# A statically ordered 32-unit graph kernel: due dates for every engine, first rows on TensorE, idle products before and between the first ones

**Chip, cores, metric.** One core of one Trainium2 chip.

## The reference

```python
# x (64, 256, 128) f32, adj (256, 256) of 0 and 1; four layers, each: x = layernorm(x + layer(x))
# layer 0, 1: attention over the graph
h = x @ W;  e = leaky(u1[i] + u2[j]);  att = softmax(masked e);  out = att @ h   # (+ x @ self_weight, or elu)
# layer 2: five gated steps
m = adj @ h
z = sigmoid(av @ w3.T + h @ u3.T + b);  r = sigmoid(av @ w4.T + h @ u3.T + b)    # av = [m, m]
h = (1 - z) * h + z * tanh(av @ w5.T + (r * h) @ u5.T + b)
# layer 3: x, adj x, adj^2 x, adj^3 x (twice), each times its own weight, summed
```

All products are in f32. A step of layer 2 needs the step before it, so one unit alone leaves TensorE waiting for ScalarE (ACT) and VectorE (DVE); many units at once fill it.

## The kernel before

Two of the 64 graphs make a unit, so there are 32; seven are in work at a time, each in a "lane" of buffers. The kernel doesn't emit instructions in program order. It notes every operation as a task with an engine, a guessed duration and its dependences, plays them through a small list scheduler, and emits each engine's instructions in the order that comes out. On the chip each engine then follows its order, whatever really happens.

```python
LATENCY = {"pe": 500, "dve": 400, "act": 400, "pool": 500, "sp": 4000}       # the planner's guesses, ns
# Plan.run, at each moment of planned time
            for e, tasks in ready.items():
                if free[e] > now:
                    continue
                fit = [t for t in tasks if t.at <= now and len(t.takes) <= len(self.free_banks)]
                if not fit:
                    continue
                t = min(fit, key=key)
# ... cut ...
    def first(t):                                  # the key: the oldest unit first
        if t.rank is not None:
            return (0, t.rank)
        late = t.unit - (NU - LANES)
        if late >= 0 and t.layer > 1:
            return (1, t.step + late * LEAD)
        return (0, t.unit - (LANES if t.layer < 2 and t.unit >= LANES else 0))
```

Layers 0 and 1 need a row of 512 numbers on all partitions. Units 0 and 1 make it with TensorE; later ones send it to DRAM and read it back. Likewise a "far" unit turns its state between steps by DVE in 32x32 blocks and by DRAM; a near one (0, 1 and the last) by TensorE.

```python
    def far(u):
        return DIRECT <= u < NU - NEAR             # DIRECT = 2, NEAR = 1
    def on_all(u, t, row, src, view):
        if u >= DIRECT:
            to_row(row, src, view, G)              # SBUF to DRAM
            from_row(t, row)                       # DRAM to all partitions
            return t, ...
        ps = bank()
        for g in range(G):
            add(PE, 110, lambda g=g: nc.tensor.transpose(...))
        return ps, ...
```

The softmax here doesn't subtract the row's maximum and nothing guards it: scores larger than these inputs give would overflow.

## Time and profile before

| | kernel before |
|---|---|
| median of 3 runs | 1450.38 us (1449.82 to 1453.53) |
| PE records, share of the span busy | 5617, 98% |
| streaming work of these records | 1399.3 us |
| lost in the first 60 us | 23.8 us |
| lost from 60 us to the last matmul | 18.5 us |
| from the last matmul to the end | 6.6 us |

How to read it: an f32 product stands in the trace as two records (a transpose as one). In a full stream a record of N columns takes N/1.2 + 2.1 ns (512: 429 ns, 256: 215 ns), read off from start to start; a one-column record 0.10 us. The streaming work is all records by this price, and "lost" is a stretch of the span less the work in it. Cutting a stretch at an edge makes an error of up to half a us. I call this the stage account; idle products are not counted as work. In the lines, PEld is TensorE's weight load, POOL is GpSimd, SP the engine that issues most DMAs, L-numbers are lines of that run's kernel.py; ps is a PSUM bank, in which TensorE puts its results, and esd a small tile of layer 0 from which layer 1 makes its row. (The prediction's 24.5 and 49 were an earlier, coarser count of the 23.8 and 48.9.) The lines of the profile are in the prediction. This one is the first product of a layer 2 on PE's timeline (start, duration, group):

```profile
59.00 1.12 PE L695 MATMUL ps<-xT,gT 128*128 128x512 f32 x2
```

### The profile page before, as it was taken

Reading aid. Unit: us, or ns where it says so; the run is one execution under the profiler, and the core shown is the slowest. Engines: PE = TensorE matmul, PEld = TensorE weight load, DVE = VectorE, ACT = ScalarE, POOL = GpSimd, SP = SyncE. Lnnn points to the kernel's source line nnn. Section 1 sums busy time; section 2 is a strip of 40 time slices with the busy share of each in tenths; the row PEclk is TensorE's granted clock in tenths of the full one; section 3 lists DMA queues with packets and bytes.
Section 4 is the critical chain, followed back from the end, with each engine's and each line's share of the span. In section 5 each row is a group of like instructions: output and inputs, shape, how many; then the busy total and the mean of one; then the engine's idle time right before and its main releaser. Section 6 shows DMA issues by size and latency. Waiting matters only on the chain.

```text
span 1448.2 us, 18393 instructions
## 1 busy us (share of the span) xinstructions
PE 1416.8 (98%) x5617; PEld 952.5 (66%) x5617; DVE 1116.6 (77%) x2598; ACT 724.5 (50%) x1372; POOL 144.8 (10%) x134
## 2 busy tenths in 40 slices
PE   7899999999999999999999999999999999999998
PEld 6565766566667666666666666666666666665666
DVE  6965788678886887878897887888778888767665
ACT  5664375445553645545544545455455445554431
POOL 0100101001011010010111000111000101000011
PEclk9999999999999999999999999999999999999999
DMA  6201334545455435554544545453554454443232
GB/s 149 47 22 30 73 81 102 119 100 115 98 118 127 96 89 114 118 122 98 110 106 110 112 92 126 105 111 86 122 116 90 106 107 99 96 106 80 66 95 66
DMA packets 516162, 142.12 MB, mean 98 GB/s; under 512 B 446176, under 2 KB 482272, under 8 KB 516064
## 3 DMA queue, kind: packets, MB, share of 16 engines
q1 hardware_dynamic: 515264, 140.42, 43.4%
q8 instruction: 45, 0.74, 0.2%
q10 hardware_dynamic: 800, 0.52, 0.1%
q14 instruction: 53, 0.43, 0.1%
HBM read 79.01 MB, written 61.85 MB: 97 GB/s over the span
## 4 chain that ended last, share of the span: by engine, by line
PE 92%; DVE 4%; ACT 2%; DMA 1%; issue 1%; SPq 1%; POOLq 0%; POOL 0%; DVEq 0%; ACTq 0%
PE ps L695 45%; PE ps L675 22%; PE ps L781 8%; PE ps L637 4%; PE ps L788 4%; PE ps L607 3%; PE ps L540 2%; PE ps L651 2%; PE ps L602 2%; DMA u<-rowu 0%; PE ps L750 0%; ACT p L585 0%; DVE st L500 0%; PE ps L447 0%; ACT e L626 0%
## 5 line engine op out<-in xcount | busy, mean ns | idle before, releaser
L695 PE MATMUL ps<-m,gT 128*128 128x512 f32 x960 | 462.0, 594 | 3.6 <-ACT m L691 2.9
L695 PEld LDWEIGHTS ps<-m,gT 128*128 128x128 f32 x960 | 177.5, 190 | 163.8 <-issue 136.6
L505 POOL TENSOR_TENSOR rstd<-ve,nhalf 128x4 f32<-128x4 f32 x128 | 144.1, 1128 | 1298.2 <-DVE ve L502 1152.6
L675 PE MATMUL ps<-adjTp,ht 128*128 128x256 f32 x928 | 230.6, 379 | 0.6 <-DVE x L510 0.6
L675 PEld LDWEIGHTS ps<-adjTp,ht 128*128 128x128 f32 x928 | 175.0, 190 | 79.5 <-issue 58.4
L714 DVE TENSOR_TENSOR p<-p,xT 128x512 f32<-128x512 f32 x160 | 109.6, 685 | 110.5 <-ACT p L708 110.2
L710 ACT ACTIVATE e<-ps,bias 128x512 f32<-128x512 f32 x160 | 109.8, 687 | 147.9 <-PE ps L695 147.9
L701 ACT ACTIVATE e<-ps,bias 128x512 f32<-128x512 f32 x160 | 109.8, 687 | 115.2 <-PE ps L695 114.8
L691 ACT COPY m<-ps 128x512 f32<-128x512 f32 x160 | 93.3, 584 | 145.5 <-PE ps L675 142.8
L695 PE MATMUL ps<-e,u5T 128*128 128x512 f32 x320 | 162.5, 593 | 0.2
L695 PE MATMUL ps<-xT,gT 128*128 128x512 f32 x320 | 162.0, 593 | 0.6 <-DVE xT L717 0.5
L703 DVE SCALAR_TENSOR_TENSOR e<-e,xT 128x512 f32<-128x512 f32 x160 | 109.4, 685 | 53.9 <-ACT e L701 53.1
L708 ACT ACTIVATE p<-ps,bias 128x512 f32<-128x512 f32 x160 | 109.9, 687 | 64.5 <-PE ps L695 63.4
L675 PE MATMUL ps<-adjT,x 128*128 128x256 f32 x512 | 127.7, 379 | 0.0
L715 DVE SCALAR_TENSOR_TENSOR p<-e,p 128x512 f32<-128x512 f32 x160 | 109.4, 685 | 7.9 <-ACT e L710 5.5
L675 PEld LDWEIGHTS ps<-adjT,x 128*128 128x128 f32 x512 | 95.4, 191 | 30.3 <-issue 19.2
L717 DVE SCALAR_TENSOR_TENSOR xT<-p,xT 128x512 f32<-128x512 f32 x160 | 109.3, 685 | 2.5
L695 PEld LDWEIGHTS ps<-e,u5T 128*128 128x128 f32 x320 | 60.0, 190 | 54.7 <-issue 44.4
L500 DVE BATCH_NORM_STATS2 st<-ps 128x6 f32<-128x256 f32 x128 | 53.7, 426 | 54.8 <-PE ps L788 44.3
L695 PEld LDWEIGHTS ps<-xT,gT 128*128 128x128 f32 x320 | 59.1, 190 | 43.1 <-issue 30.2
L626 ACT ACTIVATE e<-m,esd 128x256 f32<-128x256 f32 x120 | 86.8, 761 | 0.0
L725 DVE STREAM_TRANSPOSE p<-xT 128x512 f32<-128x512 f32 x116 | 81.6, 705 | 1.4
(137 smaller groups left out, 1841.4 us busy)
## 6 DMA issues: line engine op xcount, KB each, us to landing
hb<-p SPq DMA_DIRECT2D x174, 256.0 KB, 2.1
ht<-hb SPq DMA_DIRECT2D x464, 64.0 KB, 2.5
m<-row SPq DMA_DIRECT2D x60, 256.0 KB, 3.7
xT<-hb SPq DMA_DIRECT2D x232, 64.0 KB, 2.5
out_dram<-x SPq DMA_DIRECT2D x32, 256.0 KB, 2.3
hb<-p SPq DMA_DIRECT2D x116, 64.0 KB, 1.8
ht<-hb SPq DMA_DIRECT2D x29, 256.0 KB, 2.9
z<-in_x_dram SPq DMA_DIRECT2D x100, 64.0 KB, 2.4
```

The costliest lines, as they stand in the source:

```text
L505: add(POOL, 1050, lambda: nc.gpsimd.tensor_tensor(rstd.ap, ve.ap, nhalf.ap, op=ALU.pow), (ve, nhalf), (rstd,))
L675: add(PE, mm_ns(N), lambda b=b, mc=mc: nc.tensor.matmul(ps.ap[:, b * N : (b + 1) * N], lhs(b, mc), mat.ap[:, mc, :], start=(mc == 0), stop ...
L691: add(ACT, 500, lambda ps_m=ps_m: nc.scalar.copy(m.ap, ps_m.ap), (ps_m,), (m,))
L695: add(PE, mm_ns(T), lambda: nc.tensor.matmul(ps.ap, w(), rhs.ap, start=start, stop=stop, skip_group_check=True), (c, rhs), (ps,))
L701: add(ACT, 600, lambda ps_g=ps_g: nc.scalar.activation(r.ap, ps_g.ap, AF.Tanh, bias=bias2.ap[:, 1:2], scale=0.5), (ps_g, bias2), (r,))
L703: add(DVE, 600, lambda h=h: nc.vector.scalar_tensor_tensor(r.ap, r.ap, 1.0, h.ap, op0=ALU.add, op1=ALU.mult), (r, h), (r,))
L708: add(ACT, 600, lambda ps_v=ps_v: nc.scalar.activation(v.ap, ps_v.ap, AF.Tanh, bias=bias2.ap[:, 2:3]), (ps_v, bias2), (v,))
L710: add(ACT, 600, lambda ps_g=ps_g: nc.scalar.activation(z.ap, ps_g.ap, AF.Tanh, bias=bias2.ap[:, 0:1], scale=0.5), (ps_g, bias2), (z,))
L714: add(DVE, 600, lambda h=h: nc.vector.tensor_sub(v.ap, v.ap, h.ap), (v, h), (v,))
L715: add(DVE, 600, lambda: nc.vector.scalar_tensor_tensor(v.ap, z.ap, 1.0, v.ap, op0=ALU.add, op1=ALU.mult), (v, z), (v,))
L717: add(DVE, 600, lambda h=h, new=new: nc.vector.scalar_tensor_tensor(new.ap, v.ap, 0.5, h.ap, op0=ALU.mult, op1=ALU.add), (v, h), (new,))
L781: add(PE, mm_ns(N), lambda k=k, src=src, c=c, b=b: nc.tensor.matmul(view(c)[:, :, b, :], bn(src.ap)[:, b, c * P : (c + 1) * P], w3.ap[:, k ...
```

## The change

The intent: order all engines by due dates, so that units keep an even distance and none starves, and close ranks at the end; give the first units a straighter way (rows, loads, constants); keep TensorE's clock up with idle products; tell the planner which writes to one tile don't wait for each other.

```diff
-NEAR = 1
+NEAR = 2
+PERIOD = 43e3
+TAIL = 0.1
+PACE = 1.9
+PACE_GATED = 1.56
+HOLD = 80
+DIRECT_ROWS = 4
@@ Plan.run: a due date for each task of a new unit
+                for t in self.tasks[seen:]:
+                    t.due = max([d.due + (PACE_GATED if t.layer == 2 else PACE) * (d.ns + (
+                        d.wait + self.LATENCY["sp" if d.dma else d.eng] if d.dma or d.eng != t.eng else self.OWN[t.eng]))
+                        for d in t.deps if d.unit == t.unit], default=0.0)
@@ first(t): the key
-        late = t.unit - (NU - LANES)
-        if late >= 0 and t.layer > 1:
-            return (1, t.step + late * LEAD)
-        return (0, t.unit - (LANES if t.layer < 2 and t.unit >= LANES else 0))
+        if t.unit < 0:
+            return t.due - 1e6
+        return (t.unit - (1 - TAIL) * max(t.unit - (NU - LANES), 0)) * PERIOD + t.due
@@ loads: x of unit 0 first on ACT's queue, ahead of adj; x of units 7 to 13 later
-            if not k and u + LANES < NU:
-                load_x(u + LANES)
+            if k == (1 if u < LANES else 0) and u + LANES < NU:
+                load_x(u + LANES, after=[plan.tasks[-1]] if k else ())
@@ rows of units 2 and 3 by TensorE
-        if u >= DIRECT:
+        if u >= DIRECT_ROWS:
@@ idle products, ident by ident, 256 columns: four at the start, six in layer 1 of unit 0 at the lowest priority
+    warm(4)
+            warm(6, [plan.tasks[-1]])
@@ in thirteen places: writes of pieces of one tile are one group
-                (e, nm), (p, s))
+                (e, nm), (p, s), group=ps_)
... HOLD, waits of loads and the order of constants cut ...
```

## The prediction

> **What bounds the kernel now.** I read the page's busy table first, then the stages, then PE's waits, then the engines that PE waits for.
>
> ```profile
> PE 1416.8 (98%) x5617; PEld 952.5 (66%) x5617; DVE 1116.6 (77%) x2598; ACT 724.5 (50%) x1372; POOL 144.8 (10%) x134
> PE 92%; DVE 4%; ACT 2%; DMA 1%; issue 1%; SPq 1%; POOLq 0%; POOL 0%; DVEq 0%; ACTq 0%
> ```
>
> TensorE is the bound: 98% busy, and 92% of the chain that ended last. But busy spans of matmuls overlap, so I price the stream by its cadence. The timeline of PE in mid-kernel gives it (start, duration, group, count):
>
> ```profile
> 601.40 3.62 PE L675 MATMUL ps<-adjTp,ht 128*128 128x256 f32 x16
> 604.86 3.60 PE L695 MATMUL ps<-m,gT 128*128 128x512 f32 x8
> 608.29 1.07 PE L540 MATMUL ps<-wx,xT 128*128 128x133 f32 x8
> ```
>
> From start to start, a record of 512 columns takes (608.29-604.86)/8 = 0.429 us, one of 256 takes 3.46/16 = 0.216, one of about 130 takes 0.112. Transposes in a run of 13 near 17 us are 0.109 apart. The groups by form count 1600 records of 512, 2568 of 256, 1280 of 129 to 133, some 150 transposes and small ones, 16 of one column (0.10 each): 686 + 553 + 142 + 16 + 2 = 1399 us of pure streaming. The span is 1448.2, so **49 us are lost**, and only those can be won. Where, the stages say (columns: window, length, then busy us and counts of PE, PEld, DVE, ACT, POOL, then clock, DMA share, GB/s):
>
> ```profile
> 0.00:10.00 10.00, 5.75 (x30) 5.63 (x31) 4.00 (x18) 3.53 (x5) 0.70 (x6) 1.00 0.72 197
> 10.00:30.00 20.00, 19.10 (x165) 18.22 (x163) 15.61 (x67) 11.56 (x39) 1.02 (x1) 1.00 0.62 130
> 30.00:60.00 30.00, 17.76 (x97) 14.31 (x98) 25.97 (x85) 15.17 (x44) 4.40 (x4) 0.83 0.42 75
> 60.00:100.00 40.00, 40.00 (x171) 26.68 (x170) 29.00 (x71) 28.09 (x57) 3.19 (x3) 1.00 0.06 21
> 100.00:1200.00 1100.00, 1092.65 (x4269) 727.77 (x4268) 873.85 (x1999) 557.25 (x1040) 111.21 (x99) 1.00 0.46 103
> 1200.00:1440.00 240.00, 239.97 (x887) 158.79 (x887) 164.06 (x351) 108.92 (x190) 22.24 (x19) 1.00 0.38 88
> 1440.00:1448.20 8.20, 1.59 (x8) 1.06 (x6) 4.14 (x13) 0.00 (x0) 2.02 (x2) 0.80 0.21 65
> ```
>
> Pricing each stage's records with the cadences, I get 35.5 us of work in the first 60 (24.5 lost), about 18.5 lost from 60 to 1440 (nearly all of it between 140 and 1200, in gaps under 1 us), and 6.6 from the last matmul to the end. From 1200 to 1440 nothing is lost, so the old order already ends full. The start is the largest piece, and its waits have names:
>
> ```profile
> PE ps L490 <- DVE esd L612: 5.4, 2, 5.1
> PE ps L303 <- DMA adj_t<-in_adj_dram: 4.2, 1, 4.2
> PE ps L447 <- DVE x L514: 3.9, 2, 3.4
> PE ps L637 <- DVE p L630: 2.4, 2, 1.9
> ```
>
> Behind the 5.1 us wait at 30 us stands a DMA. The waits of DVE and of ACT up to 60 us, and the chain there:
>
> ```profile
> DVE d L559 <- DMA u<-rowu: 3.0, 2, 2.5
> ...
> ACT p L585 <- DVE nm L583: 6.4, 2, 3.3
> ...
> 29.87 4.36 DMA u<-rowu
> ```
>
> The rows of units 2 and 3 go out to DRAM and come back. The SP queue puts them among the loads of later units, they land late, DVE stands before unit 3's small sum with the last step of unit 2's maximum behind it, ACT stands before unit 2's softmax, which needs that maximum, and unit 0's ready exponential waits behind that on ACT (it starts at 35.10, its inputs were there at 31.46). So the first unit reaches layer 2, where TensorE's work is, only at 54 us.
>
> **What the Trainium skill says.** (1) "TensorE: Matmul & The Clock Gate", Part 1: the array runs at 1.2 GHz by default and at 2.4 after about 3.4 us of sustained work, and one idle window sends it back. The trace agrees: the first transposes are 0.21 us apart until 7.9 us and 0.11 later, and the granted clock is 0.69 from 30 to 35 and 0.50 from 35 to 40, after the gap of 5.1. (2) The same page, Part 2, "Back-to-back issue gap": N/2.4 + 2.5 ns. A record here is two such passes: 512/1.2 + 2.5 = 429 ns, as measured, so steady matmuls have no slack to give. [...]Here a 2 KB row takes 2.4 and the 3.8 KB gather 3.2, so a round trip of two is near 6 us, plus the queue. (4) "Advanced Engine Details and Errata", "Sequencer Loop": queued instructions wait for their semaphores. The trace shows what that costs when the order is wrong: the exponential above.
>
> **The change part by part.** The arithmetic of 29 units is untouched; only order moves.
>
> *Added PE work.* NEAR 2 lets unit 30 turn by PE instead of by DVE and DRAM: two turns of 4 transposes and five steps of 4, 28 x 0.109 = 3.1 us. DIRECT_ROWS 4 makes the rows of units 2 and 3 by PE: 2 units x 2 rows x 4 = 16 transposes, 1.7 us, and 16 one-column records, 1.6 us. Sum **+6.4 us**, all on the bound engine. The ten idle products are 20 records x 0.216 = 4.3 us at full clock; four come before any data has landed, and six have the lowest rank in the order, so I count them as lying in idle time, +0. PE should count 5617+28+32+20 = 5697 records.
>
> *Taken off the start.* The rows of units 2 and 3 lose 14 SP issues (about 6 us of queue) and both round trips. The loads for units 7 to 13 wait until layer 1 of the lane's unit instead of layer 0. That takes away the 5.1 us wait and the throttle it brings (about 10 us at a half or less, of which the records ran 4 to 5: some 2.5 us). The x load of unit 0 goes ahead of the adjacency on ACT's queue; the first matmul may come no earlier than 4 us, since adjacency still needs 3.4 from issue, so perhaps 0.5 later. Four warm products from about 1.4 us on put the full clock at about 5 to 6 us instead of 7.9: about 1 us. The write groups only let the planner know that pieces of a tile don't wait for each other, so its order fits the chip better; 1 to 2 us on the first unit's chain. A limit stays: layers 0 and 1 cost DVE about 14 us per unit and PE about 6.6, so until the first unit is in layer 2, PE can't be full. If that comes at about 44 instead of 54, PE's loss falls by about the same. I take **24.5 to 14, -10.5 us**.
>
> *Middle.* Due dates with 43 us between units spread seven units over their phases, where the old key let the oldest unit take everything and then starve. The real PE period is 1399/32 = 43.7, so the pace fits. But only 18.5 us are there, in small waits. I take a third to a half: **18.5 to 10.5, -8 us**.
>
> *End.* It was full until the last matmul, and the last statistics, POOL power, four scalings and a store (2.3 us to land) still follow. Unit 30 near gives shorter steps, which the new tail, with units 4.3 us apart, needs; it buys no more than is lost now: **0**.
>
> Sum: 6.4 - 10.5 - 8 + 0 = -12.1 us, so 1450.4 goes to **1438**; I round it down by one for the reach of the clock, **1437 us** (0.9% faster).
>
> **Rivals.** (a) *The added transposes and products eat the gain.* For it: PE is the bound for 1200 us, and every added record there is paid in full. Against: they sum to 6.4, the lost start to 24.5. If the start wins only 5 and the middle nothing: about 1451. (b) *Due dates starve the middle.* For it: durations and latencies are the planner's guesses (a DMA is taken as 4 us), engines run in the order given, and DVE at 79% from 100 to 1200 has little slack; a tail of seven units at once makes DVE wait. Against: the old order used the same guesses and lost 1.7% there. If loss there doubles: 1455 to 1465. (c) *DVE sets the start.* It is 87% busy from 30 to 60 and 100% from 50 to 60, which speaks for it: then removing the DMA wait saves only some 5 us and PE goes on waiting for DVE: 1443. (d) *Everything fits:* start loss 10, middle 4, end 6: 1405 + 20 + 2 of launch = 1427. Even this is not 2%, which would be 1421.4, or all but some 14 us of the lost time gone.
>
> **Range and chances.** The lower end is (d) less a little, the upper end (a): 1426 to 1450. Faster by over 2% needs more than the profile has to give once the added work is paid: 0.05. Slower by over 2% (1479) would need 29 us of new waits in an order that was surely tried: 0.03. Within 2%: 0.92.
>
> **What would show it right or wrong.** Right: PE at about 5697 records; no clock below 0.9 after 10 us; no wait of PE for the esd row over 2 us; the first layer-2 matmul with the 512-column gate weights near 48 instead of 59 us; work in the first 60 us at 44 to 48 us instead of 35.5; PE busy 100 to 1200 at over 1095 of 1100. Wrong: DVE at 100% through 20 to 60 with PE waiting for it (c); new waits of PE for ACT's copies or DVE's new state in the middle (b); PE gaps after 1350, where there were none; idle products standing between real ones (a). A store or a DVE queue at the end longer than 7 us would void the zero there.

## More of the kernel before

Times are device microseconds (us) of one execution, medians of the runs. Runs of one call share a chip and the runs of the kernel before on it.

## The result

1439.39 us median of 4 runs (1438.70 to 1440.57) against 1450.27 of the kernel before: ratio 0.9921, 95% interval 0.9904 to 0.9938. So 0.8% faster, within 2%. (A ratio is the mean time of one kernel's runs over that of the other's of the same rounds, so not quite the ratio of the medians.) The profiled run is the slowest of the four, 1440.57.

Busy time of PE, and the chain that ended last, of the changed kernel:

```profile
PE 1423.5 (99%) x5697; PEld 962.9 (67%) x5697; DVE 1113.1 (77%) x2589; ACT 722.6 (50%) x1378; POOL 143.5 (10%) x134
PE 97%; DVE 1%; ACT 1%; issue 0%; POOL 0%; POOLq 0%; DVEq 0%
```

PE is busy for longer in a shorter span (4.3 us of it are the ten idle products, priced by cadence), and the chain is now 97% PE: DMA has gone from it, and DVE fell from 4% to 1%. The stages (window, length, then busy us and counts of PE, PEld, DVE, ACT, POOL, then clock, DMA share, GB/s):

```profile
0.00:10.00 10.00, 8.64 (x38) 7.72 (x39) 3.85 (x17) 2.94 (x4) 0.70 (x6) 1.00 0.68 193
10.00:30.00 20.00, 19.70 (x173) 19.25 (x172) 17.39 (x69) 12.57 (x39) 1.73 (x2) 1.00 0.24 69
30.00:60.00 30.00, 29.07 (x165) 22.80 (x164) 27.99 (x84) 20.69 (x54) 5.49 (x5) 1.00 0.31 55
...
100.00:1200.00 1100.00, 1094.36 (x4283) 731.45 (x4282) 878.84 (x2012) 554.96 (x1041) 110.86 (x100) 1.00 0.48 105
```

The third line is where the change shows: from 30 to 60 us PE goes from 17.76 busy to 29.07 of 30 (some 2.6 of them the six idle products), and the clock from 0.83 to 1.00. The last has hardly moved (1092.65 before). PE's longest waits over the whole span:

```profile
PE ps L725 <- DVE esd L638: 2.7, 1, 2.7
PE ps L725 <- ACT m L721: 2.0, 3, 0.8
PE ps L663 <- DVE p L656: 1.7, 2, 1.0
PE ps L299 <- POOL ident masks.py:199: 1.4, 1, 1.4
```

The waits for the esd row at 30 us and for the state at 54 are gone, and the one for the adjacency at the start is filled by idle products. From PE's timeline, the idle products (the groups with ident alone as operand) and the first product of a layer 2:

```profile
1.36 3.78 PE L299 MATMUL ps<-ident 128*128 128x256 f32 x8 [1.36 <-POOL ident masks.py:199]
...
35.06 2.75 PE L299 MATMUL ps<-ident 128*128 128x256 f32 x12
38.60 1.99 PE L663 MATMUL ps<-p,x 128*128 128x256 f32 x8 [0.79 <-DVE p L656]
...
47.02 1.02 PE L725 MATMUL ps<-xT,gT 128*128 128x512 f32 x2
```

Layer 2 starts at 47.0 us instead of 59.0. One new thing stands in the middle, the 2.7 us wait of the list above. Timeline and windows of PE there:

```profile
1192.25 1.02 PE L818 MATMUL ps<-e,a2T 128*128 128x256 f32 x4
1195.99 2.08 PE L725 MATMUL ps<-xT,gT 128*128 128x512 f32 x2 [2.72 <-DVE esd L638]
1197.86 1.51 PE L725 MATMUL ps<-m,gT 128*128 128x512 f32 x2
1199.20 1.89 PE L705 MATMUL ps<-adjTp,ht 128*128 128x256 f32 x8
```

```profile
1194.00:1196.00 2.00, 0.01 (x1) 0.01 (x1) 1.35 (x8) 0.00 (x0) 1.68 (x2) 0.85 0.35 88
1196.00:1198.00 2.00, 2.00 (x3) 0.97 (x4) 1.28 (x5) 0.00 (x0) 0.00 (x0) 0.50 0.04 1
```

PE stands 2.7 us until DVE has finished a layer 0 of another unit (its esd is the last reader of that unit's PSUM tile; a replay of the planner, whose order matches PE's records in the trace one by one, gives the waiting product, of unit 28, the very bank that unit 29's layer 0 held before). GpSimd's two powers in a row (1.68 us in the first window) are on the way to it. Then the granted clock is 0.50 and the next four records of 512 columns take 3.21 us instead of 1.72: some 4.2 us for one bad moment of the order. It is no accident of this run: a wait of 2.2 to 2.7 us for esd stands between 1191 and 1199 us in the profiles of experiments 4, 5, 6 and 10 too.

### The profile page after: what moved, and what is told of

It reads as the page before. It is cut to its first block, busy times and chain, and to the rows that moved or that the text cites. A ratio compares the mean times of both kernels' runs of the same rounds, so it can differ in the third digit from the quotient of the medians.

```text
span 1438.8 us, 18453 instructions
## 1 busy us (share of the span) xinstructions
PE 1423.5 (99%) x5697; PEld 962.9 (67%) x5697; DVE 1113.1 (77%) x2589; ACT 722.6 (50%) x1378; POOL 143.5 (10%) x134
## 4 chain that ended last, share of the span: by engine, by line
PE 97%; DVE 1%; ACT 1%; issue 0%; POOL 0%; POOLq 0%; DVEq 0%
PE ps L725 48%; PE ps L705 23%; PE ps L811 8%; PE ps L633 4%; PE ps L663 4%; PE ps L818 4%; PE ps L677 2%; PE ps L628 2%; PE ps L566 2%; PE ps L780 1%; PE ps L471 0%; ACT e L652 0%; DVE st L525 0%; PE ps L299 0%; PE ps L514 0%
## 5 line engine op out<-in xcount | busy, mean ns | idle before, releaser
L705 PE MATMUL ps<-adjTp,ht 128*128 128x256 f32 x896 | 222.6, 379 | 0.0
L705 PEld LDWEIGHTS ps<-adjTp,ht 128*128 128x128 f32 x896 | 169.6, 190 | 62.2 <-issue 40.9
L725 PEld LDWEIGHTS ps<-e,u5T 128*128 128x128 f32 x320 | 59.9, 190 | 38.1 <-issue 26.3
L525 DVE BATCH_NORM_STATS2 st<-ps 128x6 f32<-128x256 f32 x128 | 51.9, 425 | 40.9 <-PE ps L818 21.2
L652 ACT ACTIVATE e<-m,esd 128x256 f32<-128x256 f32 x112 | 80.4, 761 | 0.7 <-DMA m<-row 0.7
L755 DVE STREAM_TRANSPOSE p<-xT 128x512 f32<-128x512 f32 x112 | 78.3, 700 | 1.2
```

Of the source, the lines that this page charges most:

```text
L705: add(PE, mm_ns(N), lambda b=b, mc=mc: nc.tensor.matmul(ps.ap[:, b * N : (b + 1) * N], lhs(b, mc), mat.ap[:, mc, :], start=(mc == 0), stop ...
L725: add(PE, mm_ns(T), lambda: nc.tensor.matmul(ps.ap, w(), rhs.ap, start=start, stop=stop, skip_group_check=True), (c, rhs), (ps,))
```

## The experiments

The stage account of all kernels. "Planner's idle" is the idle time of TensorE between 60 us and its last matmul in the planner's own account, without a chip: I replayed the planner of each kernel for it.

| kernel | median us | ratio to before | work | lost to 60 us | lost 60 to last matmul | of it to 1200 | after it | planner's idle |
|---|---|---|---|---|---|---|---|---|
| before | 1450.38 | 1 | 1399.3 | 23.8 | 18.5 | 16.7 | 6.6 | 36.5 |
| changed | 1439.39 | 0.9921 | 1405.7 | 11.7 | 14.4 | 13.0 | 7.0 | 26.0 |
| 1 old key in the changed | 1470.85 | 1.0129 | 1405.7 | 16.0 | 42.3 | 40.9 | 6.6 | 57.8 |
| 2 new key alone in the old | 1473.66 | 1.0150 | 1399.3 | 24.9 | 41.2 | 8.6 | 6.5 | 63.5 |
| 3 rows of units 2, 3 back | 1460.65 | 1.0060 | 1402.3 | 16.8 | 31.9 | 9.6 | 6.8 | 63.7 |
| 4 no idle products | 1442.78 | 0.9937 | 1405.7 | 13.7 | 14.7 | 12.1 | 7.0 | 26.0 |
| 5 one near unit | 1443.22 | 0.9940 | 1402.6 | 11.2 | 21.1 | 11.2 | 6.4 | 38.6 |
| 6 loads of units 7 to 13 early | 1439.52 | 0.9915 | 1405.7 | 10.8 | 14.3 | 12.1 | 7.0 | 27.1 |
| 7 no groups | 1446.96 | 0.9965 | 1405.7 | 12.5 | 20.1 | 7.4 | 6.6 | 38.1 |
| 8 other constants | 1432.09 | 0.9865 | 1404.0 | 14.0 | 6.2 | 3.5 | 6.7 | 16.1 |
| 9 rows alone in the old | 1461.12 | 1.0059 | 1402.6 | 16.5 | 34.0 | 32.5 | 6.3 | 50.5 |
| 10 pace 1.85 | 1467.34 | 1.0113 | 1405.7 | 11.7 | 49.7 | 11.2 | 6.7 | 67.7 |
| 11 best constants | 1433.52 | 0.9873 | 1405.7 | 10.6 | 7.6 | 4.8 | 7.0 | 10.9 |

The kernel before took 1451.43 in the call of 1 to 4, 1450.89 in that of 5 to 8 and 1452.90 in that of 9 to 11, so kernels of different calls are compared by ratio.

A caution for the whole table: undoing any part gives the planner another problem, and it draws a whole new order. The time of an ablation is therefore not the price of the part. The stage nearest to the part is.

### 1. The old key

```diff
-        return (t.unit - (1 - TAIL) * max(t.unit - (NU - LANES), 0)) * PERIOD + t.due
+        late = t.unit - (NU - LANES)
+        if late >= 0 and t.layer > 1:
+            return (1, t.step + late * LEAD)
+        return (0, t.unit - (LANES if t.layer < 2 and t.unit >= LANES else 0))
```

> The changed kernel with the old priority key put back (oldest unit first), everything else of the change kept. Theory A, the rows and loads of the first units give the start and the key gives only the middle: loss in the first 60 us stays near 12 us (changed kernel 11.7, kernel before 23.8), loss from 60 us to the last matmul goes back from 14.4 to about 18.5, time about 1443. Rival B, the due dates give most of everything: start loss back above 19, time 1449 or more. Rival C, the key does nothing: 1439 within 2.

Measured 1470.85. None of the three had it: the start lies between A and B (16.0), and the middle is far worse than in the kernel before. One window of it, with PE's busy time first:

```profile
60.00:1200.00 1140.00, 1116.87 (x4336) 740.69 (x4337) 885.70 (x2041) 572.90 (x1087) 118.46 (x99) 1.00 0.45 98
```

With everything else of the change in place, the oldest-first key loses 23 us there by busy time alone. So with these parts and constants the key is needed: without it the rest of the change makes the middle worse.

### 2. The new key alone

```diff
 # kernel before, with t.due, PERIOD, TAIL, PACE, PACE_GATED and
+        return (t.unit - (1 - TAIL) * max(t.unit - (NU - LANES), 0)) * PERIOD + t.due
```

> The kernel before with the due dates as its key and nothing else of the change (rows of units 2 and 3 still through DRAM, old loads, no idle products, one near unit). Theory A: start loss stays above 19 us, middle loss 14 or 15, no added PE work, time about 1446. Rival B: start loss near 13, time about 1435 to 1438, faster than the whole change because the 6.4 us of added work are missing. Rival D: the tail of the new key needs the second near unit, then gaps appear after 1400 us and the time is above 1450.

Measured 1473.66, the slowest median of all. The time refutes A and B; D said where to look. Two stages of it:

```profile
60.00:1200.00 1140.00, 1137.91 (x4450) 759.10 (x4449) 895.94 (x2064) 586.81 (x1106) 108.52 (x99) 1.00 0.45 100
...
1350.00:1471.90 121.90, 96.77 (x338) 61.87 (x337) 58.08 (x125) 35.53 (x60) 10.01 (x9) 0.93 0.20 47
```

Up to 1200 us due dates do what they are for: 8.6 us lost instead of the old key's 16.7. Then the last seven units close up and PE stands 25 us in the last 122 (6.5 of them after its last matmul). Its longest waits from 1300 on are for DVE's normalised state (6.4 us), for a turned unit to land from DRAM (5.3) and for DVE's new state (4.2 in three).

```profile
PE ps L683 <- DVE x L522: 6.4, 1, 6.4
PE ps L789 <- DMA xT<-hb: 5.3, 1, 5.3
```

The start is no better than before (24.9). That the missing second near unit is the cause, as D had it, is not shown: experiment 5 has one near unit too and lost 9.9 us after 1200, against 32.6 here.

### 3. Rows of units 2 and 3 through DRAM again

```diff
-DIRECT_ROWS = 4
+DIRECT_ROWS = 2
```

> The changed kernel with the rows of units 2 and 3 through DRAM again. Theory A: start loss rises from 11.7 to 17 or more, 3.3 us of PE work fall away, time about 1442, and a wait of PE for the esd row or of DVE for the gather of over 2 us is back. Rival B or E, the key orders around the DRAM trips, or the later loads alone freed the queue: start loss about 12, time about 1436, so those two direct units were paid for nothing.

Measured 1460.65. The start rose to 16.8, near A's 17. The time is far above A's 1442 because the new order lost 22 us after 1200, which says nothing on rows. No single wait for a row or the gather over 2 us came back, so the mechanism of A is not shown by this run, only its size.

### 4. No idle products

```diff
-    warm(4)
-            warm(6, [plan.tasks[-1]])
+            pass
```

> The changed kernel without its ten idle products. Theory: they hold the clock; without the four the clock comes up about 2 us later (start loss +1), without the six a gap of over 3 us near 35 to 38 us halves the clock for one window of 3.4 us (+1.7): start loss, idle products not counted as work, 11.7 to about 14, time about 1441.5. Rival: nothing on the path runs in those microseconds, time 1439.4 within 1.

Measured 1442.78 (ratio 0.9937 against 0.9921), with 2.0 us more lost at the start and the rest as it was. The size is as the theory said, but the two intervals (0.9921 to 0.9954, 0.9904 to 0.9938) overlap, so it is the trace that shows the mechanism. PE's timeline, and the clock from 40 to 45:

```profile
39.46 2.54 PE L662 MATMUL ps<-p,x 128*128 128x256 f32 x8 [3.37 <-DVE p L655]
```

```profile
40.00:45.00 5.00, 5.00 (x26) 4.66 (x25) 4.50 (x20) 3.21 (x13) 1.32 (x1) 0.66 0.06 3
```

Without the six, PE stands 3.37 us, and the clock is 0.66 of full afterwards. With them it stands 0.79 and runs at 1.00. How much the four at the start help is left to chance: in the profiled run of the changed kernel records go at the full rate from about 7.4 us, in that of experiment 8 too, in those of experiments 6 and 11, with the same four, already at or just after the first real product (4.6 and about 5.0). Without them it was about 10, in the kernel before 7.9. The first real products of the changed kernel and of experiment 11:

```profile
4.93 0.63 PE L342 MATMUL ps<-centre,w 128*128 128x128 f32 x2
4.93 0.42 PE L342 MATMUL ps<-centre,w 128*128 128x128 f32 x2
```

By the clock records of the traces the rise came at 4.2 to 7.6 us in the nine profiled runs with the four, at 7.7 to 10.1 in the four without. At half rate those 3.4 us are up to 1.7 us of loss, so start losses of single profiles that differ by less than that (the 0.8 of experiment 7, say) prove little.

### 5. One near unit

```diff
-NEAR = 2
+NEAR = 1
```

> The changed kernel with only the last unit near, unit 30 turning through DVE and DRAM again. Theory F, the new tail of seven units needs short steps at the end: PE work falls by 3.1 us, start stays 11.7, but PE gaps of 8 to 15 us appear after 1350 us, time about 1446 to 1452, with a wait of PE for a DMA landing (turned unit or its steps). Rival: one near unit is enough, time 1436, the 3.1 us were paid for nothing.

Measured 1443.22. 3.1 us of work fall away and 6.7 come back as loss (after 1200 it rose from 1.4 to 9.9), so the second near unit paid here, by less than I expected; the intervals overlap (0.9923 to 0.9956, 0.9904 to 0.9938), and the order is another, so that it pays in general is not shown. The mechanism was another: not a DMA (PE waited 0.3 us for one) but one gap, for DVE's normalised state:

```profile
1412.40 0.33 PE L471 MATMUL ps<-ident,x 128*128 128x128 f32 x1 [3.21 <-DVE x L539]
```

After it records again took longer than their price until about 1418: some 1.8 us more.

### 6. Loads of units 7 to 13 early

```diff
-            if k == (1 if u < LANES else 0) and u + LANES < NU:
-                load_x(u + LANES, after=[plan.tasks[-1]] if k else ())
+            if not k and u + LANES < NU:
+                load_x(u + LANES)
```

> The changed kernel with the x loads of units 7 to 13 issued after layer 0 of the lane's first unit again, instead of after layer 1. Theory: with the rows of four units made by PE, the SP queue has little to carry before 40 us, so loads in it no longer hold anything up: start loss 11.7 to 13, time 1439 to 1441. Rival, the queue of SP was the cause: start loss 15 or more and a wait of over 2 us for a row, time 1443 or more.

Measured 1439.52, ratio 0.9915: the same as the changed kernel. With the rows off the queue, this part of the change carries nothing.

### 7. No groups

```diff
-                (e, nm), (p, s), group=ps_)
+                (e, nm), (p, s))          # and so in all places
```

> The changed kernel without the groups that tell the planner that pieces of one tile do not wait for each other. No instruction changes, only the order that comes out. Theory G: an order planned with false waits loses on the chip: start loss 14 to 15, middle loss up by 5 to 10 us, time 1446 to 1452. Rival: the order hardly differs, 1439 to 1441.

Measured 1446.96. Not one instruction differs from the changed kernel's, only their order. The start lost 0.8 more, less than I expected, the rest 5.7 more. G holds in size for time and middle.

### 8. Other constants

```diff
-PERIOD = 43e3
-TAIL = 0.1
-PACE = 1.9
-PACE_GATED = 1.56
-DIRECT_ROWS = 4
+PERIOD = 43.5e3
+TAIL = 0.3
+PACE = 1.7
+PACE_GATED = 1.66
+DIRECT_ROWS = 3
```

> The changed kernel with other constants of the due dates: 43.5 us between units, tail 0.3, pace 1.7, gated pace 1.66, rows of three units direct. Chosen because in the planner's own account TensorE idles less in the middle (16 us against 26) and 2.5 us more at the start; 1.7 us of PE work fall away. Theory H, in 60 us to the last matmul the planner's account ranks orders as the chip does: middle loss 14.4 falls to about 8, start loss 11.7 rises to about 14, time about 1434 to 1436, faster than both kernels. Rival, the planner's account is fitted to the constants it has and the chip's own waits decide: 1440 to 1450.

Measured 1432.09, ratio 0.9865: faster than both kernels, and by more than the theory asked. Middle loss 6.2 instead of 14.4, start 14.0. The same window as in 1 and 2:

```profile
60.00:1200.00 1140.00, 1140.00 (x4467) 762.14 (x4466) 911.74 (x2076) 581.73 (x1099) 110.74 (x102) 1.00 0.47 103
```

PE is never seen idle in 1140 us. The mechanism of the change can do this; the changed kernel's constants didn't.

### 9. Rows alone in the kernel before

```diff
-        if u >= DIRECT:
+        if u >= DIRECT_ROWS:              # 4, in both places
```

> The kernel before with the rows of units 2 and 3 made by TensorE and nothing else of the change. If the rows alone cure the start: start loss 23.8 falls to about 14. If rows and key are both needed (undoing either in the changed kernel gave 16 to 17, the key alone gave nothing): start loss 17 to 21. The wait of PE for the esd row (5.1 us in the kernel before) should be under 2 us in both cases. Middle loss is expected to get worse, since the planner's own account of this order has 50 us of idle TensorE there against 36 for the kernel before: 25 to 35 us, so the time is 1452 to 1462.

Measured 1461.12. Start 16.5, slightly better than "both needed" said: rows alone give 7.3 of the 12.1 us. The longest wait for the esd row fell from 5.1 to 2.2 us, just above the 2 that I had named. The middle got worse as the planner's account said (34.0).

```profile
PE ps L491 <- DVE esd L613: 3.2, 2, 2.2
```

### 10. Pace 1.85

```diff
-PACE = 1.9
+PACE = 1.85
```

> The changed kernel with one constant changed by 3 per cent: pace 1.85 for 1.9. No instruction is added or removed. Theory H: the order is sensitive to its constants and the planner's account shows it (68 us of idle TensorE in the middle against 26): middle loss 35 to 45 us instead of 14.4, start 11.7 as before, time 1460 to 1472, slower than the kernel before. Rival: the due dates as such carry the gain, a small change of pace leaves 1438 to 1444.

Measured 1467.34, from 1463.55 to 1475.47, the profiled run being the slowest. The same start (11.7), the same loss to 1200 (11.2), and some 38 us lost in the last lap. PE's longest wait in total, all of it there, is for DVE's new state:

```profile
PE ps L780 <- DVE xT L747: 11.5, 4, 3.0
```

A constant changed by 3% turns 0.8% faster into 1.1% slower. Middle loss was even a little above the range, but that is the slowest run; at the median it would be some 8 us less, within it. Either way the rival is out. Waiting is not all of it: after 1200 us PE has no record for 19.8 us, and 26 busy us fall into stretches of half clock, an estimated 13 us more.

### 11. Best constants by the planner's account

```diff
-PERIOD = 43e3
-TAIL = 0.1
-PACE = 1.9
-PACE_GATED = 1.56
+PERIOD = 42.5e3
+TAIL = 0.3
+PACE = 1.7
+PACE_GATED = 1.7
```

> The changed kernel with 42.5 us between units, tail 0.3, pace 1.7, gated pace 1.7, the best of some 7000 sets by the planner's own account (11 us of idle TensorE in the middle, four direct units, start as in the changed kernel). Theory H: middle loss 3 to 5 us, start loss 11 to 12, end 7, time 1429 to 1431, a little faster than the set with 43.5, 0.3, 1.7 and 1.66 (1432.1). Rival, below some 15 us the planner's account no longer ranks: 1433 or more.

Measured 1433.52, ratio 0.9873, no different from experiment 8 within the intervals (0.9858 to 0.9888 here, 0.9850 to 0.9880 there). Start 10.6, a little below what I said, middle 7.6 instead of 3 to 5. So the rival holds: the account ranks an order of 68 against one of 26 against one of 16, but not 11 against 16.

## Why the prediction was right

**Added work: +6.4 us.** Right to the tenth: 1405.7 less 1399.3, and 5697 records, as counted. Nothing of it was hidden, as a full engine must show.

**Start: 24.5 to 14, -10.5.** Measured -12.1 (23.8 to 11.7). The size holds and the first layer 2 came at 47.0, where I had said near 48. The shares I gave were partly wrong. The four idle products were to bring the full clock at 5 to 6 us, worth 1; in this profile it came at about 7.4 instead of 7.9, worth some 0.2. The later loads, which I listed, carry nothing (experiment 6). Rows carry the most: 7.3 us alone, 5.1 when undone. The key, which I had put to the middle, is worth 4.3 us of the start when undone but nothing alone, so it seems to need the rows off the DRAM. The six idle products, which I counted as zero, keep up a clock: together with the four they are worth 2.0, some of which I had booked under the removed wait. The groups give 0.8 there, within the chance of the clock's rise. (Two slips in the working change no sum: half clock lasted 10.2 us in the kernel before and was 0.50, never less; and two passes of N/2.4 + 2.5 would be 432 ns, so 429 agrees with one fixed part for a record, not two.)

**Middle: 18.5 to 10.5, -8.** This is the term that was mis-sized: measured 18.5 to 14.4, -4.1. These missing 3.9 us, less the 1.6 that the start gave beyond its term, are nearly the whole of what the predicted sum lacks. I reasoned that due dates at the pace of PE would take a third to a half. They took about half up to 1200 us in experiment 2 (16.7 to 8.6), four fifths in experiment 8 (3.5), and in the changed kernel one stall at 1194 us with the throttle after it took some 4.2 us back. Without that the term would have come out near -8. What I had missed is that the loss of an order is not a property of its rule: the same rule loses 6.2, 14.4 or 49.7 us by its constants. The total was right with one term at half its size, and some luck: with a pace of 1.85 for 1.9, which the prediction didn't weigh, the same change gives 1467 us, outside the range.

**End: 0.** Measured +0.4. PE was full until its last matmul, without a gap after 1350.

Sum by measurement: 6.4 - 12.1 - 4.1 + 0.4 = -9.4 us, which is the difference of the two profiled spans (1448.2 and 1438.8); predicted -12.1.

**The rivals.** (a) Added work eating the gain: no, though it takes 6.4 of 15.8. (b) Due dates starving PE: not in this kernel, but it happened in experiments 2, 3 and 10, and there in the last lap, where seven units close up. I gave slower 0.03 because the order was "surely tried". That was right, and for a thin reason: these constants were evidently picked. Of 2000 random sets played through the planner (period 41 to 46 us, tail 0 to 0.6, pace 1.4 to 2.2, gated pace 1.3 to 1.9) 4.6% had less planned idle time than these. (c) DVE sets the start: no, with DVE at 27.99 and PE at 29.07 of 30 us from 30 to 60 both are nearly full. (d) Everything fits, 1427: the changed kernel didn't, experiment 8 came within 5 us of it.

**Checks that failed.** A clock below 0.9 after 10 us: yes, at 1196. PE over 1095 of 1100 from 100 to 1200: 1094.36. Work in the first 60 us was 48.3, just above the 44 to 48. No wait for the esd row over 2 us came in layer 1, but the stall at 1194 is a wait for esd, as a bank's last reader.

**What stays open.** Why some constants ruin the last lap and others don't, I have only from the waits (for DVE's state, for ACT's copies); no run isolates it. Rows and key have no clean shares, since each run of one without the other also has another order.

## What to carry to other kernels

Price the full engine's stream by its cadence, subtract it from the span, and place the rest by stage: that bounds what an order can win before anything is built. When the order of a kernel comes out of a planner, undoing a part redraws everything, so judge an ablation by the stage that the part touches, not by its time. And search the planner's constants by the planner's own account before the chip: here it told bad orders from good ones, though not every pair (experiment 3, 63.7 planned, lost less than experiment 9, 50.5), and found a further 0.6%.

## What the Trainium skill lacked or had wrong

- "TensorE: Matmul & The Clock Gate", Part 1, gives about 3.4 us of idleness, a whole window, before the clock falls. Here a gap of 2.72 us sufficed: the granted clock was 0.85 in the 2 us of the gap and 0.50 in the next 2. Nor is the gap's length what decides: one of 3.35 us in the kernel before (to 54.10) left the clock at 1.00, and so did the same 2.72 us in experiment 5. In the 13 traces the clock changes on a grid of 3.41 us. All 19 full-clock steps of this grid in which PE was busy for less than 1.35 us were followed by half clock, of those with 1.40 to 1.75 us four of eleven, of those with 1.8 or more none.
- The same page, Part 1, has the moment of warming vary by 500 ns either way with the window's phase; it doesn't say how much idle products are worth. With the same four of them (3.4 to 3.8 us) the clock rose at 4.2 to 7.6 us in nine profiled runs, against 7.7 to 8.0 in the three of the old start and 10.1 in experiment 4, all without them.
- The same page, Part 4, says that the full clock does not engage for transposes. Here, once products had raised it, 13 f32 transposes in a row (one record each) took 0.109 us each, which is twice 128 columns at 2.4 GHz plus 2.1 ns, and 0.21 us each before the clock rose. Whether transposes alone would raise it, no run shows.
- "Perfetto Trace Analysis", Identifying the Most-Contended Engine, says that pipelined matmuls look smaller in the trace. Here they look longer: 594 ns on average for a record whose neighbours start 429 ns apart.
- No page that I found treats orders drawn up beforehand for all engines. Here the order alone, with the same instructions, moved the time from 1433.5 us (experiment 11) to 1467.3 (experiment 10), more than the change itself did.
